# A convolution layer on one core: its first row transfers on another queue, the next chunk's loads ahead of them, and its accumulating stores issued later in the program

## The chip, the core and the metric

The kernel runs on one core of a Trainium2 chip. The metric is the time of one execution on the device in microseconds (us); smaller is better. The core has TensorE (PE in the profile, its weight loads PEld), VectorE (DVE), ScalarE (ACT), GpSimd (POOL) and SyncE (SP). SP, ACT and POOL can issue transfers (DMAs). In the profile "SPq" or "POOLq" is the queue of that engine, and "L1160" is line 1160 of the kernel.

## The reference

The input `x` holds 1024 pictures of 16 x 16 positions with 16 channels. Four layers of the form `x = x + layer(groupnorm(x))` follow one another: a tensor-train matrix product (layer 0), a small cellular automaton with a hidden layer of 128 (layer 1), a 3 x 3 convolution (layer 2), and a second automaton (layer 3). The change is in layer 2:

```python
def _L2_conv_ref(x, filters, bias):
    out = jax.lax.conv_general_dilated(x, filters, window_strides=(1, 1),
        padding='SAME', dimension_numbers=('NHWC', 'HWIO', 'NHWC'))
    return out + bias

x = x + _L2_conv_ref(_gn(x), L2_conv_filters, L2_conv_bias)
```

## The kernel before

**Chunks.** The batch is cut into two chunks of 512 pictures. Two large buffers in SBUF, `X0` and `X1` (128 partitions x 32 lines x 512 pictures), hold the normalized activations of a chunk. A layer runs on chunk 0 in `X0` and then on chunk 1 in `X1`. While one chunk is convolved, the other buffer is loaded with the input of the layer that comes next for it, and normalized in place. The residual stream lies in DRAM in the tensors `xf`.

**Layer 2 (`layer_conv`).** For chunk `n`, each of 16 rows `h` is computed in two halves `wh` of the row's width, as matmuls of 128 x 128 weights with up to three lines of `X` (`inner`, L1160). What crosses from one half to the other is added by `across` (L1169), whose operands are copied beforehand from `X` into small tiles `hx`. The function `halo(k)` (L1146) copies them for four rows: twelve rows of 16 partitions in six DMAs on SP's queue, and for `k = 0` also two small ones at L1156. `start()` issues `halo(0)`, and the rows 1, 5 and 9 issue the next ones. `finish(h)` (L1187) lets ACT add the bias while it moves each half of a row from PSUM to a tile `r` (L1191), of which there are six, and lets POOL issue a DMA at once that adds this tile to the residual stream in DRAM (L1192).

**Order of work.** Instructions are written in the program's order for each engine[...]. `run` (L1423) interleaves three lists: the 54 main steps of the convolution; the 16 loads of the other buffer (512 KB each), spread evenly until the share `by` of the main steps is done; and the steps of the normalization of that buffer, laid out between the shares `lo` and `hi` of the main steps, in proportion to their costs. What lies beyond the last main step is written at its end. So `by`, `lo` and `hi` only set the place of an instruction in the queues.

**The two runs of layer 2.** The first (L1536) convolves `X0` and loads and normalizes `X1` for the second; the loads come from the stream that layer 1 left, and the normalization is `norm_lines`: sums over all 16 pairs of lines (DVE L589, L592, L596), a matmul for the mean (L675), a copy of it by ACT (L636), 16 subtractions (DVE L621), squares (ACT L606) and their sum (DVE L592), a matmul for the variance (L679), a root (ACT L653) with a refinement on DVE (L659 to L663), and 16 multiplications (DVE L621). The second (L1538) convolves `X1` and loads and normalizes `X0` for layer 3 with `norm_cw`, which does the same in four quarters of eight lines each, interleaved: one mean (L704) and one variance (L708) for each quarter, then one root and, for each quarter, a matmul that spreads it (L720), a copy (L636) and four multiplications. These loads read what the first run's accumulating DMAs write, and each of them needs all 16 rows of its half. Before them `put(L3)` (L1455) loads the weights of layer 3.

**Transfers in flight.** [...]

Of the kernel before, what the change touches and what calls it, by code (L numbers as in the profile page):

```python
# [12 lines left out]
ALU = mybir.AluOpType  # L13
# [90 lines left out]
def conv_preact_kernel(ctx: ExitStack, tc: tile.TileContext, a: dict, out: bass.AP):  # L104
    nc = tc.nc
    V, A, G, T = nc.vector, nc.scalar, nc.gpsimd, nc.tensor
# [9 lines left out]
    xf = [  # L116
        [dram.tile([8, 4, P, NB], F32, tag=f"xf{l}_{n}", name=f"xf{l}_{n}") for n in range(NCH)]
        for l in range(5)
    ]
# [16 lines left out]
    def work(shape, tag, name, dt=F32):  # L136
        p, sizes = pool["sb"]
        return p.tile(shape, dt, tag=tag, name=name, bufs=sizes[tag])
# [5 lines left out]
    def psum(shape, name):  # L144
        return bank(shape, shared[0], name)
# [485 lines left out]
    def held(st, q=0):  # L631


        def copy():
            st["m", q] = work([P, NB], "s", "m")
            A.copy(st["m", q], st["p"])  # L636

        return (0, copy)
# [28 lines left out]
    def norm_lines(X, on_act=True):  # L667
        parts = [lambda l=l: X[:, l : l + 2] for l in range(0, NL, 2)]
        s1, steps = line_sum(parts, "s1", False)
        s2, more = line_sum(squares(X, 0, NL, on_act), "s2", True, not on_act)  # L670
        st = {}

        def mean():
            st["p"] = psum([P, NB], "pmean")
            T.matmul(st["p"], gm_wc, s1["s"], start=True, stop=True)  # L675

        def var():
            st["v"] = psum([P, NB], "pvar")
            T.matmul(st["v"], gm_wc, s2["s"], start=True, stop=True)  # L679

        def keep():
            st["ve"] = work([P, NB], "n", "ve")
            V.tensor_scalar(st["ve"], st["v"], GN_EPS, None, ALU.add)

        steps = steps + [5, mean, 2, held(st), 2] + each(X, 0, NL, lambda: st["m", 0], ALU.subtract)
        steps += more + [5, var, 2, keep] + rstd(st)
        return steps + by_rows(each(X, 0, NL, lambda: st["r"], ALU.mult))
# [49 lines left out]
    def norm_cw(X, on_act):  # L737


        st, N = parts_cw(X, on_act)  # L740
        sums, sq, hold = N["sums"], N["sq"], N["held"]
        mean, var, keep, spread = N["mean"], N["var"], N["keep"], N["spread"]
        steps = sums[0] + woven(sums[1], (2, mean[0]), (3, hold[0])) + [1] + sq[0]
        for q in (1, 2):
            steps += woven(
                sums[q + 1], (1, var[q - 1]), (3, keep[q - 1]), (3, mean[q]), (4, hold[q])
            ) + [2] + sq[q][:4]
            if q == 1:
                steps += sq[q][4:]
        steps += woven(sq[2][4:], (2, mean[3]), (3, hold[3]))  # L750
        steps += woven(sq[3], (2, var[2]), (4, keep[2])) + [5, var[3], 2, keep[3]]
        return steps + rstd(st) + [4] + scaled(N, range(4))
# [11 lines left out]
    def load_wc(X, src):  # L764
        return [
            lambda wh=wh, h=h: nc.sync.dma_start(X[:, 16 * wh + h : 16 * wh + h + 2], rows_wc(src, wh, h, 2))
            for wh in range(2)
            for h in range(0, S, 2)
        ]

    def load_cw(X, src):
        return [
            lambda q=q, w=w: nc.sync.dma_start(
                X[:, 8 * q + w : 8 * q + w + 2], src[w : w + 2, q].rearrange("w p b -> p w b")
            )
            for q in range(4)
            for w in range(0, 8, 2)
        ]
# [5 lines left out]
    def rows_wc(t, wh, h, n=1):  # L784

        t = t[4 * wh : 4 * wh + 4].rearrange("w q (c h) b -> (w q c) h b", h=S)
        return t[:, h : h + n]
# [349 lines left out]
    def layer_conv(X, n):  # L1137

        st = {}

        def start():
            halo(0)

        def halo(k):  # L1146
            t = st["h", k] = work([P, 4, NB], "hx", "hx")
            for wh in range(2):
                src = X[slice(97, 128, 2) if wh else slice(0, 32, 2), 16 * (1 - wh) : 16 * (1 - wh) + 16]
                for y in range(3):  # L1150
                    r0, h0 = 64 * wh + 16 * y, 4 * k + y - 1
                    lo, hi = max(h0, 0), min(h0 + 4, S)
                    nc.sync.dma_start(t[r0 : r0 + 16, lo - h0 : hi - h0], src[:, lo:hi])
                    if lo > h0:

                        nc.sync.dma_start(t[r0 : r0 + 16, 0:1], src[:, 0:1])  # L1156

        def inner(h, y):
            for wh in range(2):
                T.matmul(  # L1160
                    st["po", h][wh], conv["fw"][:, y], X[:, 16 * wh + h + y - 1],
                    start=y == max(0, 1 - h), stop=y == min(2, S - h),
                )

        def across(h):
            rows = 32 if h == S - 1 else 48
            for wh in range(2):
                cols = slice(0, 32) if wh else slice(96, 128)
                T.matmul(  # L1169
                    st["po", h][wh][cols], conv["hw"][64 * wh : 64 * wh + rows, h == 0],  # L1170
                    st["h", h // 4][64 * wh : 64 * wh + rows, h % 4], start=False, stop=False,
                )

        def first(h):
            if h % 2 == 0 and h > 0:
                finish(h - 1)
            if h % 4 == 1 and h + 4 < S:
                halo(h // 4 + 1)
            st["po", h] = [bank([P, NB], "o", "po2") for _ in range(2)]
            inner(h, max(0, 1 - h))  # L1180

        def last(h):
            inner(h, min(2, S - h))
            if h % 2 == 0 or h == S - 1:
                finish(h)

        def finish(h):  # L1187

            for wh in range(2):
                r = work([P, NB], "r", "conv")  # L1190
                A.activation(r, st["po", h][wh], AF.Identity, bias=b2)  # L1191
                G.dma_start(rows_wc(xf[2][n], wh, h), r.unsqueeze(1), accum_op=ALU.add)  # L1192

        steps = []
        for h in range(0, S, 2):
            for j in (h, h + 1):
                steps.append(lambda j=j: first(j))
                if 0 < j < S - 1:
                    steps.append(lambda j=j: inner(j, 1))
            steps += [  # L1200
                lambda h=h: (across(h), across(h + 1)), lambda h=h: last(h), lambda h=h: last(h + 1)
            ]
        return start, steps

    def layer_nca(X, n, l, L, xo=None):
# [217 lines left out]
    def run(layer, us, loads, *spans, by=0.0):  # L1423

        start, main = layer
        start()
        loads, done = list(loads), 0  # L1430
        todo = []
        for bg, lo, hi in spans:
            bg = [b if isinstance(b, tuple) else (1, b) if callable(b) else (b, None) for b in bg]
            idle = sum(b[0] for b in bg if b[1] is None) / (us * (hi - lo))
            less = min(1.0, 0.7 / idle) if idle else 1.0
            weight = sum(b[0] for b in bg if b[1] is not None)
            at = lo
            for cost, step in bg:
                if step is None:
                    at += cost * less / us  # L1440
                else:
                    todo.append((at, step))
                    at += (hi - lo) * (1 - idle * less) * cost / weight
        todo.sort(key=lambda x: x[0])
        for i, step in enumerate(main):
            step()
            part = (i + 1) / len(main)
            while done < len(loads) and done < len(loads) * part / (by or 1e-9):
                loads[done]()
                done += 1  # L1450
            while todo and (todo[0][0] < part or i == len(main) - 1):
                todo.pop(0)[1]()

    def put(L):
        return lambda: nc.sync.dma_start(pack, L["pack"])  # L1455

    X0, X1 = XN
    gn = dict(t4=3, s=3, n=2)
# [16 lines left out]
    L3, make3 = nca_weights("L3_conv_", X1[:, 16:32])  # L1475
# [42 lines left out]
    last = alone(N, 3) + rstd(nst, slice(96, 128)) + [3] + scaled(N, [3])  # L1518
    nca_sb = dict(t4=2, s=3, n=2, wq=5, mask=1, f=5, hid=8, u=2, r=4, nx=1)
    nca_ps = dict(h=6, o=2)  # L1520
    conv_sb, conv_ps = dict(gn, s=3, r=6, hx=3), dict(o=6, m=2)
    on_vector[0] = True
    with ExitStack() as es:
        shared[0] = "o"
# [8 lines left out]
    with ExitStack() as es:  # L1533
        shared[0] = "m"
        stage(es, conv_sb, conv_ps)
        run(layer_conv(X0, 0), 108, load_wc(X1, xf[2][1]), (norm_lines(X1), 0.09, 1.1), by=0.12)  # L1536
        run(
            layer_conv(X1, 1), 108, [put(L3)] + load_cw(X0, xf[3][0]), (norm_cw(X0, True), 0.09, 1.04), by=0.12  # L1538
        )
    with ExitStack() as es:  # L1540
        shared[0] = "o"
# [41 lines left out]
```

## Time and profile before

| what | value |
|---|---|
| time, median of three runs | 3199.06 us (3191.19, 3199.06, 3200.33) |
| the profiled execution | 3191.8 us |
| its span, first to last instruction | 3190.1 us |
| PE busy | 3058.5 us (96%) |
| DVE, ACT, POOL busy | 1785.6, 1018.3, 670.6 us |
| mean granted clock of PE | 0.98 |
| layer 2, first run (PE, 2339.7 to 2464.0 us) | 124.3 us, PE busy 105.1, DVE 78.9, ACT 37.4; DMA share 0.78 |
| layer 2, second run (PE, 2464.0 to 2591.5 us) | 127.5 us, PE busy 111.6, DVE 79.6, ACT 41.1; DMA share 0.72 |
| the 64 accumulating DMAs (L1192) | 256 KB each, 0.87 us of POOL each to issue, 6.1 us to landing (median) |

"DMA share" is the mean busy share of the core's 16 DMA engines. All times inside the execution count from the start of its span. The limits of the two runs are those of PE's own matmuls: from the first matmul of row 0 to the first matmul of what follows.

### The profile page before, as it was taken

How to read it: one execution, taken by the hardware profiler on the slowest of the kernel's cores; microseconds unless marked ns; L12 is line 12 of the kernel's file. 1: busy time of each engine (PE TensorE's matmuls, PEld its weight loads, DVE VectorE, ACT ScalarE, POOL GpSimd, SP SyncE). 2: the span in 40 equal slices, each digit the busy share in tenths (PEclk: the TensorE clock that was granted, in tenths of full speed). 3: DMA queues.
4: the chain of work that ended last, by engine and by line, in shares of the span. 5: the costliest groups of instructions: out<-in, count | busy, mean ns of one | idle time of the engine just before them, and what ended most of it. 6: DMA issues, size and time to landing. Idle time of an engine off the chain costs nothing.

```text
span 3190.1 us, 37179 instructions
## 1 busy us (share of the span) xinstructions
PE 3058.5 (96%) x13874; PEld 1260.3 (40%) x13874; DVE 1785.6 (56%) x2378; ACT 1018.3 (32%) x1690; POOL 670.6 (21%) x706
## 2 busy tenths in 40 slices
PE   7899899999999999999999999999979899999996
PEld 5444333444444444444444433333323233333332
DVE  5255345755554555544556678558757647754222
ACT  4331221100001000000111166666624356655553
POOL 1116532200000000000000034435432124432221
PEclk8999999999999999999999999999989999999998
DMA  7535545443333433322222254454476765433445
GB/s 283 201 142 97 121 101 160 133 144 104 104 109 132 146 116 104 104 98 96 90 95 90 76 168 133 129 167 154 139 192 110 185 139 173 136 92 115 128 137 186
DMA packets 243299, 424.77 MB, mean 133 GB/s; under 512 B 37844, under 2 KB 91952, under 8 KB 239408
## 3 DMA queue, kind: packets, MB, share of 16 engines
q1 hardware_dynamic: 217824, 368.63, 35.5%
q0 software_dynamic: 24480, 53.48, 8.3%
q8 instruction: 110, 1.80, 0.2%
q14 instruction: 69, 0.57, 0.1%
q10 hardware_dynamic: 816, 0.30, 0.0%
HBM read 238.78 MB, written 165.60 MB: 127 GB/s over the span
## 4 chain that ended last, share of the span: by engine, by line
issue 46%; PE 31%; POOL 8%; DMA 4%; DVE 2%; SPq 1%; ACT 1%; POOLq 0%; DVEq 0%; ACTq 0%
PE ph L1410 11%; PE po L1078 10%; PE po L1263 4%; POOL res L1313 4%; POOL u L1312 4%; PE po L1160 2%; DMA xn<-xf 1%; PE L_conv_pe L382 1%; SPq L941 1%; DVE xn L621 1%; DMA hx<-xn 1%; PE pw L1001 1%; PE ptout L948 1%; DVE sq L592 1%; POOL L_conv_wy L394 0%
## 5 line engine op out<-in xcount | busy, mean ns | idle before, releaser
L1078 PE MATMUL po<-xn,w 128*128 128x512 f32 x3584 | 1584.3, 598 | 4.6 <-DVE xn L892 4.6
L1078 PEld LDWEIGHTS po<-xn,w 128*128 128x128 f32 x3584 | 669.9, 190 | 852.6 <-issue 833.7
L1413 ACT ACTIVATE hid<-ph,pack 128x512 f32<-128x512 f32 x1024 | 653.9, 686 | 429.2 <-PE ph L1410 308.4
L1114 DVE TENSOR_TENSOR r<-r,po 128x512 f32<-128x512 f32 x576 | 377.8, 683 | 499.0 <-PE po L1078 476.3
L1312 POOL TENSOR_TENSOR u<-u,mask 128x512 f32<-128x512 f32 x128 | 202.5, 1582 | 1858.9 <-DMA nx<-xn 1241.7
L1410 PE MATMUL ph<-xn,wq 32*128 32x512 f32 x3664 | 573.1, 613 | 1.5 <-DMA wq<-L_conv_wy 1.5
L1006 ACT COPY w<-pw 128x512 f32<-128x512 f32 (+1 forms) x320 | 150.6, 558 | 1194.0 <-issue 970.4
L1410 PEld LDWEIGHTS ph<-xn,wq 32*128 32x128 f32 x3664 | 228.6, 184 | 263.3 <-issue 231.4
L1410 PE MATMUL ph<-xn,pack 32*128 32x512 f32 x1288 | 302.2, 631 | 4.5 <-ACT hid L1413 3.2
L1263 PE MATMUL po<-hid,pack 128*32 128x512 f32 x2048 | 283.0, 609 | 1.2 <-DVE u L1275 0.9
L1019 DVE TENSOR_TENSOR w<-w 128x512 f32<-128x512 f32 x320 | 211.2, 684 | 115.2 <-ACT w L1006 114.7
L621 DVE TENSOR_TENSOR xn<-xn,m 128x1024 f32<-128x1024 f32 x160 | 225.9, 1461 | 47.1 <-ACT m L636 47.1
L1313 POOL TENSOR_TENSOR res<-res,u 128x512 f32<-128x512 f32 x128 | 215.2, 1681 | 17.0 <-PE po L1263 2.7
L1275 DVE SCALAR_TENSOR_TENSOR u<-po,pack,xn 128x512 f32<-128x512 f32 x128 | 95.9, 749 | 157.6 <-PE po L1263 150.9
L1160 PE MATMUL po<-xn,convw 128*128 128x512 f32 x368 | 168.5, 609 | 0.0
L1410 PEld LDWEIGHTS ph<-xn,pack 32*128 32x128 f32 x1288 | 114.5, 187 | 100.7 <-issue 61.7
L1114 DVE TENSOR_TENSOR xn<-xn,po 128x512 f32<-128x512 f32 x96 | 64.3, 684 | 125.9 <-PE po L1078 125.8
L592 DVE TENSOR_TENSOR sq<-sq 128x1024 f32<-128x1024 f32 x78 | 110.6, 1418 | 15.2 <-ACT sq L606 12.0
L1263 PEld LDWEIGHTS po<-hid,pack 128*32 128x32 f32 x2048 | 42.9, 108 | 189.7 <-issue 137.4
L394 POOL DMA_DIRECT2D L_conv_wy<-xn x160 | 89.0, 563 | 99.0 <-ACT xn L152 90.7
L1160 PEld LDWEIGHTS po<-xn,convw 128*128 128x128 f32 x368 | 69.3, 193 | 99.3 <-issue 96.7
L592 DVE TENSOR_TENSOR s<-s,xn 128x1024 f32<-128x1024 f32 x60 | 86.4, 1441 | 29.1 <-DMA xn<-xf 27.9
(163 smaller groups left out, 1776.9 us busy)
## 6 DMA issues: line engine op xcount, KB each, us to landing
xf<-r SPq DMA_DIRECT2D x112, 512.0 KB, 3.8
xn<-xf SPq DMA_DIRECT2D x96, 512.0 KB, 5.1
r<-xf SPq DMA_DIRECT2D x80, 512.0 KB, 4.5
wq<-L_conv_wy SPq DMA_DIRECT2D x192, 192.0 KB, 2.8
res<-xf SPq DMA_DIRECT2D x128, 256.0 KB, 3.0
xf<-res SPq DMA_DIRECT2D x96, 256.0 KB, 2.0
res<-xr SPq DMA_DIRECT2D x256, 64.0 KB, 2.8
xf<-conv POOLq DMA_DIRECT2D x64, 256.0 KB, 6.1
```

Source lines behind the costliest of these rows:

```text
L592: return lambda: V.tensor_tensor(st["t"], st["t"], p(), ALU.add)
L621: V.tensor_tensor(part, part, m().unsqueeze(1).broadcast_to([P, 2, NB]), op)
L1006: A.copy(w[:, k0:4, :, 32 * r : 32 * r + 32].rearrange("p k t (v o) -> p v (k t) o", v=2), pw[r],)
L1019: V.tensor_tensor(w[:, k], w[:, x], w[:, y], ALU.add if sign > 0 else ALU.subtract)
L1078: T.matmul(po, st["w", u][:, matrix, t], x, start=t == 0, stop=t == 3)
L1114: V.tensor_tensor(r[at], r[at], po, ALU.add if sign > 0 else ALU.subtract)
L1160: T.matmul(st["po", h][wh], conv["fw"][:, y], X[:, 16 * wh + h + y - 1], start=y == max(0, 1 - h), stop=y == min(2, S - h),)
L1263: T.matmul(po[32 * j : 32 * j + 32], nca["w1"][:, v], hid[j], start=v == 0, stop=v == 1)
L1312: G.tensor_tensor(u, u, st["m"][:, w2], ALU.mult)
L1313: G.tensor_tensor(r, r, u, ALU.add)
L1410: T.matmul(ph, w, x, start=k == 0, stop=k == len(tiles) - 1)
L1413: A.activation(h, ph, AF.Relu, bias=nca["bt"][:, r : r + 1])
```

## The change

- `halo(0)` of each of the two runs is issued from ACT's queue and no longer from SP's. The later ones stay on SP.
- `finish(h)` no longer writes the accumulating DMAs behind the bias at once. It puts them into a list. Those of row 0 and 1 are written into POOL's queue when row 5 is finished, then four at each of the rows 5 to 9, and from row 10 on two at each row. There are twelve tiles `r` and not six.
- The loads are written within the first 7% of the main steps and not 12%.
- In the second run `put(L3)` stands behind the 16 loads and not ahead of them.
- The normalization of the first run is laid out up to 1.08 and not 1.10, that of the second up to 1.10 and not 1.04.

```diff
         def start():
-            halo(0)
+            halo(0, A)
-        def halo(k):
+        def halo(k, queue=nc.sync):
...
-                    nc.sync.dma_start(t[r0 : r0 + 16, lo - h0 : hi - h0], src[:, lo:hi])
+                    queue.dma_start(t[r0 : r0 + 16, lo - h0 : hi - h0], src[:, lo:hi])
                     if lo > h0:
-                        nc.sync.dma_start(t[r0 : r0 + 16, 0:1], src[:, 0:1])
+                        queue.dma_start(t[r0 : r0 + 16, 0:1], src[:, 0:1])
...
+        waiting = []
         def finish(h):
             for wh in range(2):
                 r = work([P, NB], "r", "conv")
                 A.activation(r, st["po", h][wh], AF.Identity, bias=b2)
-                G.dma_start(rows_wc(xf[2][n], wh, h), r.unsqueeze(1), accum_op=ALU.add)
+                waiting.append((rows_wc(xf[2][n], wh, h), r.unsqueeze(1)))
+            while waiting and 2 * h + 2 - len(waiting) < 4 * (h - 4):
+                G.dma_start(*waiting.pop(0), accum_op=ALU.add)
...
-    conv_sb, conv_ps = dict(gn, s=3, r=6, hx=3), dict(o=6, m=2)
+    conv_sb, conv_ps = dict(gn, s=3, r=12, hx=3), dict(o=6, m=2)
...
-        run(layer_conv(X0, 0), 108, load_wc(X1, xf[2][1]), (norm_lines(X1), 0.09, 1.1), by=0.12)
+        run(layer_conv(X0, 0), 108, load_wc(X1, xf[2][1]), (norm_lines(X1), 0.09, 1.08), by=0.07)
         run(
-            layer_conv(X1, 1), 108, [put(L3)] + load_cw(X0, xf[3][0]), (norm_cw(X0, True), 0.09, 1.04), by=0.12
+            layer_conv(X1, 1), 108, load_cw(X0, xf[3][0]) + [put(L3)], (norm_cw(X0, True), 0.09, 1.1), by=0.07
         )
```

## The prediction

> **What bounds the kernel now.** I read the page first: PE is busy 96% of the span, so what can be won is what PE waits. Then the waits of PE in the stretch of layer 2 (2330 to 2600 us):
>
> ```profile
> PE pmean L675 <- DVE s1s L596: 12.4, 1, 12.4
> PE pmean L704 <- DVE s1s L596: 11.0, 1, 11.0
> PE po L1169 <- DMA hx<-xn: 6.2, 2, 5.4
> PE pvar L708 <- DVE s2s L596: 4.9, 2, 2.6
> PE pvar L679 <- DVE s2s L596: 0.6, 1, 0.6
> ```
>
> 35 us in all: twice PE stands at the mean of the other chunk's normalization, because DVE has not summed all lines, and at the start it stands for the halo. Why is DVE late? Its timeline in the first run:
>
> ```profile
> 2364.43 2.50 DVE L592 TENSOR_TENSOR s<-s,xn 128x1024 f32<-128x1024 f32 x2 [5.88 <-DMA xn<-xf]
> 2368.18 1.22 DVE L592 TENSOR_TENSOR s<-s,xn 128x1024 f32<-128x1024 f32 x1 [1.25 <-DMA xn<-xf]
> ...
> 2391.78 1.22 DVE L592 TENSOR_TENSOR s<-s,xn 128x1024 f32<-128x1024 f32 x1 [1.43 <-DMA xn<-xf]
> ```
>
> It waits for loads. Eleven loads (6th to 16th) take 2391.8 - 2365.7 = 26.1 us, 2.37 each. The stretches of time say why (the last three columns are PE's granted clock, DMA share and GB/s):
>
> ```profile
> 2345.00:2350.00 5.00, 0.11 (x1) 0.00 (x0) 0.00 (x0) 0.00 (x0) 0.00 (x0) 1.00 0.79 180
> 2350.00:2355.00 5.00, 3.69 (x7) 0.69 (x8) 0.00 (x0) 0.00 (x0) 0.00 (x0) 0.52 0.93 249
> 2365.00:2370.00 5.00, 5.00 (x16) 1.85 (x16) 3.10 (x3) 0.00 (x0) 0.00 (x0) 1.00 1.08 308
> 2490.00:2495.00 5.00, 4.06 (x5) 1.85 (x6) 3.96 (x5) 0.58 (x1) 0.00 (x0) 0.50 1.04 387
> ```
>
> The DMA engines are full. Loads alone (last line) run at 387 GB/s, 1.35 us for 512 KB; the eight accumulating DMAs of rows 0 to 3 took 18.6% of the 16 engines over 61 us (queues in 2339 to 2400), 1.42 each; 11 x 1.35 + 8 x 1.42 = 26.2, the 26.1 seen. A halo is about 0.79 x 5 us = 4.0 of DMA time (first line, an upper estimate). Last, the queues that issue:
>
> ```profile
> 2343.17 1.27 POOL L1313 TENSOR_TENSOR res<-res,u 128x512 f32<-128x512 f32 x1
> 2359.87 0.95 POOL L1192 DMA_DIRECT2D xf<-conv  x1 [15.44 <-ACT conv L1191]
> 2361.58 2.61 POOL L1192 DMA_DIRECT2D xf<-conv  x3 [0.77 <-ACT conv L1191]
> 2373.02 3.50 POOL L1192 DMA_DIRECT2D xf<-conv  x4 [8.83 <-ACT conv L1191]
> ```
>
> Between layer 1's last multiply-add and layer 3, POOL has nothing but these DMAs, and each goes out about 0.3 us after the ACT instruction that fills its tile (the first ran 2358.87 to 2359.56).
>
> [...]
>
> **The change, part by part.**
>
> *Held rows.* The code only moves the 20 DMAs of rows 0 to 9 later in program order. POOL's queue holds nothing between them. Each waits for its own tile, not for row 5: that a wait is for the needed work alone, and not for all that is written earlier, is seen at the second run's first halo, written behind all 16 multiplications (L621): it went out at 2454.99, after the fourth, 13 us ahead of the last. So POOL should reach the DMA of row 0 as early as before, and issue it when its tile is filled: **no row is held**, 0 us. The 8 x 1.42 = 11.4 us of contention stay. Were rows held, they would go (first rival). Twelve tiles in place of six remove no wait: none of ACT's idle time was for a tile.
>
> *First halo by ACT, first run.* SP stood behind the last stores (L1315) until 2344.78. ACT is free at 2338.7, but the tile `hx` is the first one of its pool and takes the place of layer 1's first, the mask, last read by POOL until 2343.1. So the eight issues start at 2343.2, between bounds of 2338.7 and 2344.9: 1.7 earlier. Issues took 0.57 each on SP (2344.87 to 2349.82 for eight less the last); ACT's 16 of the start of the kernel took 0.32 to 0.56. I take 0.6 with waits. The last lands some 1 us earlier at best, since loads now run beside it; PE's 6.2 us shrink by 0 to 1.7. That is worth nothing yet, for PE stands later at the mean.
>
> *Loads first.* Loads may start as the halo DMAs before them land (eight in flight), from 2345.8 and not 2349.86, five of them ahead of `halo(1)` instead of three. DMA engines fill 1.3 us sooner (0.79 and 0.93 become 1 in two stretches) and the halo begins 1.7 sooner: total work is the same, so the last load lands 3 us earlier, at 2388.5, and PE's mean comes at 2390.6 instead of 2393.9: **-3.3 us**. PE stood there from 2381.4 before, now from 2380.7 or so: 10 us of wait stay.
>
> *1.08 in the first run.* Laying the steps out by their costs, the variance (0.768 before, 0.754 now, of 54 steps) stands one step earlier, ahead of `first(12)` (4 passes of 0.44 us). PE waits for DVE's sum there (0.57 before), so the step it had done before the wait comes after it: **+1.8**. DVE's chain sum, subtract, square is continuous and moves by -3.3. Run 1 ends at T = 2464.0 - 3.3 + 1.8 = 2462.5.
>
> *First halo by ACT, second run.* SP issued it from 2454.99 on, as soon as DVE had multiplied the rows, 14 us before PE needed it (2469.28). ACT comes to it only behind the bias of row 15, 1.0 us after T (2463.43 to 2464.98 before). Behind it on ACT is nothing until `finish(0)`. Eight issues take 4.9 us; the DMAs share the engines with the last four accumulations (5.7 us): together about 9.7 us, so they land near T + 10.5, while PE needs them at T + 5.3: a **new wait of about 5 us**, with a half-clock start that I put at 0 to 2.5 us.
>
> *Loads of the second run.* They wait for the last accumulations (2470.5 before, T + 6.5). The halo delays these by 1 to 4 us, `put(L3)`, moved behind, gives about 1 back; I take T + 7.8 = 2470.3, as before. Four loads of the first quarter now go together: 2.3 + 4 x 1.35 + 1, then 2.3 us of DVE: first sum at 2481 (before 2490.9). PE reaches the mean at T + 5.3 + 5 + 1.8 + 8.8 + 1 = 2484.4: **the 11.0 us go**. What is late next: the second quarter. DVE subtracts only after its sum, and loads 5 to 8, `halo(1)` and the accumulations of rows 0 and 1 are the same work as before: 8 x 1.35 + 4.0 + 5.7 = 20.5 us, with 2.3 to the first landing and 2.3 of DVE, so this ends near 2495.4 against 2496.2. Squares then save 2.7 (before, ACT stood behind row 2's bias until 2499.69): variance at 2505.2 against 2507.9. PE arrives at 2498: **a new wait of 7 us**. The gain of the mean is handed on to the variance.
>
> *1.10 in the second run.* The first two variances stand one step later (0.278 against 0.264), so PE has one step more behind it: -1.8. From the first variance to the second DVE, ACT and PE alternate: 16.9 us, as before (17.05), plus 2.5 if PE restarts at half clock. I take it: second variance at 2524.6 (before 2524.9). The rest, 66.5 us before, is 64.8: PE ends at 2589.4 (before 2591.5). The spreads move three steps later (0.829 to 0.875), so the third quarter's multiplications start only after the last row's bias; layer 3's first matmuls need the first of them some 1.3 us after PE's end: +1.
>
> **Sum:** -2.1 + 1 = about -1; with no half-clock restart -3.5. I take -2: 3191.8 - 2 = 3190 for an execution like the profiled one, whose span is 1.7 us less. The median lies 7.3 above it, and the three runs stand at two levels, so the same -2 gives 3197 there; I write 3195. A measurement of this kernel can tell about 0.3%, 9.6 us.
>
> **The rivals.**
> - *Rows are held after all* (POOL meets a wait that I don't see). For: it is what the edit is meant to do. Against: POOL's empty queue. Then loads run alone: run 1's mean at 2380.7, -13; the second quarter's sum 5.7 plus about 4 sooner: in all -20, 3172 to 3179. Chance 0.10.
> - *Slower.* The halo of the second run goes ahead of the last accumulations in full, 4 us, so all loads and DVE's chain come 4 us later, and run 1 gains nothing while its +1.8 stays, and +1.3 at layer 3: +7, with a cold start +9.6; 3199 to 3207. It decides from accumulations that land later than T + 10. For: both lists of DMAs are issued in the same 4 us. [...] Chance 0.20.
> - *Lighter DMA.* The halo is an upper estimate; if it costs 2.5 us and PE stays warm, -8, 3184 to 3191. Chance 0.10.
> - My forecast, -6 to +3: 0.60.
>
> Faster by over 0.3%: 0.10 and 0.04 of the third; slower: 0.12 of the second and the forecast's edge; the rest, 0.74, within. The range 3182 to 3206 leaves out held rows and the ends of the others.
>
> **What would show it.** Right: POOL's first L1192 near 2359 and not after row 5; the mean of run 1 at 2390; the halo wait in run 2 at 5 us, L704 no longer waiting, L708 waiting 7. Wrong: POOL's first L1192 after 2385 with loads at 1.35 us each.

## The result, and the profile after

The changed kernel takes 3199.35 us in the median of four runs (3198.74 to 3201.45), the kernel before beside it 3198.85 in four: the ratio is 1.0008, with an interval of 0.999 to 1.0025. This measurement cannot tell it from no change. I had said 3195, and had given 0.74 to a change of less than 0.3%. The total is as forecast; the way there is not.

PE's waits in layer 2 of the changed kernel (2330 to 2610 us; line, what it waited for, us in total, times, longest):

```profile
PE po L1169 <- DMA hx<-xn: 31.7, 4, 13.9
PE pvar L708 <- DVE s2s L596: 3.2, 2, 2.2
PE pvar L679 <- DVE s2s L596: 2.2, 1, 2.2
PE ph L1414 <- DVE xn L621: 1.1, 1, 1.1
```

The 23.4 us of waits at the two means (L675, L704) are gone. But `across` (L1169) now waits 31.7 us for its halo, and had waited 6.2. The sum of all waits is 38.2 us against 35.1. PE's timeline has the four waits, and behind them the means that no longer wait:

```profile
2360.23 1.91 PE L1169 MATMUL po<-hx,convw 48*32 48x512 f32 x2 [13.86 <-DMA hx<-xn]
...
2365.26 3.59 PE L1169 MATMUL po<-hx,convw 48*32 48x512 f32 x6 [3.11 <-DMA hx<-xn]
...
2393.07 1.02 PE L675 MATMUL pmean<-s1s,gm_wc 128*128 128x512 f32 x2
...
2473.94 1.50 PE L1169 MATMUL po<-hx,convw 48*32 48x512 f32 x2 [4.13 <-DMA hx<-xn]
...
2486.05 3.59 PE L1169 MATMUL po<-hx,convw 48*32 48x512 f32 x6 [10.62 <-DMA hx<-xn]
...
2500.85 1.02 PE L704 MATMUL pmean<-s1s,gm_cw 128*128 128x512 f32 x2
```

The halo waits are 17.0 us in the first run and 14.75 in the second. I had forecast 4.5 to 6.2 and 5. ACT's queue in the first run (start, length):

```profile
2344.39 0.60 ACTq L1153 DMA_DIRECT2D hx<-xn  x1
2345.02 0.59 ACTq L1156 DMA_DIRECT2D hx<-xn  x1
2345.66 7.83 ACTq L1153 DMA_DIRECT2D hx<-xn  x3
2353.52 0.60 ACTq L1156 DMA_DIRECT2D hx<-xn  x1
2354.16 4.73 ACTq L1153 DMA_DIRECT2D hx<-xn  x2
```

ACT starts when I said, but eight issues of 0.6 us take until 2358.9: within the group of three (its third to fifth) it stands some 6 us, in the last pair (its seventh and eighth) 3.5. Meanwhile SP has issued five loads in 2.6 us, from 2346.13 on. And POOL, whose queue was to hold the rows, issues the first of them:

```profile
2371.93 0.95 POOL L1196 DMA_DIRECT2D xf<-conv  x1 [26.23 <-ACT conv L1193]
```

ACT's first bias ended at 2371.62; POOL issued 0.31 us later. No row is held.

### The profile page after: what moved, and what is told of

It reads as the page before. It is cut to its first block, busy times and chain, and to the rows that moved or that the text cites. A ratio compares the mean times of both kernels' runs of the same rounds, so it can differ in the third digit from the quotient of the medians.

```text
span 3197.5 us, 37179 instructions
## 1 busy us (share of the span) xinstructions
PE 3063.8 (96%) x13874; PEld 1261.1 (39%) x13874; DVE 1785.4 (56%) x2378; ACT 1018.0 (32%) x1690; POOL 669.7 (21%) x706
## 4 chain that ended last, share of the span: by engine, by line
issue 49%; PE 30%; POOL 9%; DMA 3%; SPq 1%; DVE 1%; ACT 0%; POOLq 0%; DVEq 0%; ACTq 0%
PE ph L1414 11%; PE po L1078 9%; PE po L1267 4%; POOL u L1316 3%; POOL res L1317 3%; PE po L1160 2%; PE L_conv_pe L382 1%; DMA L_conv_wy<-xn 1%; POOL xf L1196 1%; SPq L941 1%; PE ptout L948 1%; PE po L1169 1%; PE pw L1001 1%; POOL L_conv_wy L394 0%; PE ptx L1326 0%
## 5 line engine op out<-in xcount | busy, mean ns | idle before, releaser
L1414 PE MATMUL ph<-xn,wq 32*128 32x512 f32 x3664 | 574.4, 614 | 1.4 <-DMA wq<-L_conv_wy 1.4
L1414 PEld LDWEIGHTS ph<-xn,wq 32*128 32x128 f32 x3664 | 228.7, 184 | 263.0 <-issue 232.0
L1414 PE MATMUL ph<-xn,pack 32*128 32x512 f32 x1288 | 304.4, 633 | 5.8 <-ACT hid L1417 3.6
L1414 PEld LDWEIGHTS ph<-xn,pack 32*128 32x128 f32 x1288 | 114.9, 187 | 102.2 <-issue 62.5
L592 DVE TENSOR_TENSOR sq<-sq 128x1024 f32<-128x1024 f32 x78 | 110.7, 1419 | 16.4 <-ACT sq L606 13.1
L592 DVE TENSOR_TENSOR s<-s,xn 128x1024 f32<-128x1024 f32 x60 | 86.6, 1443 | 21.5 <-DMA xn<-xf 20.1
```

The costliest lines, as they stand in the source:

```text
L592: return lambda: V.tensor_tensor(st["t"], st["t"], p(), ALU.add)
L1414: T.matmul(ph, w, x, start=k == 0, stop=k == len(tiles) - 1)
```

## The experiments

Twelve kernels, each against the kernel before. A profiled execution's whole time is a poor witness here: row 0 of layer 2 began anywhere from 2334.3 to 2345.5 us, though none of the edits touches the layers ahead of it. So the table has, beside the ratio of times, the length of layer 2 from its first `inner` to its last, and PE's waits in it (what layer 3 waits at its start, up to 1.1 us, is not counted). The same kernel, profiled twice (e4, e8), differed there by 3.3 us, so a smaller difference of two rows says nothing. The waits are in us; "halo" is L1169, "means" L675 and L704, "variances" L679 and L708.

| kernel | ratio of times, interval | layer 2 | halo | means | variances | sum |
|---|---|---|---|---|---|---|
| before | 1 | 251.8 | 6.2 | 23.4 | 5.5 | 35.1 |
| changed | 1.0008 [0.999, 1.0025] | 254.6 | 31.7 | 0 | 5.4 | 37.1 |
| e1, halo on SP | 0.9989 [0.9982, 0.9997] | 250.3 | 6.2 | 16.0 | 11.2 | 33.4 |
| e2, before + halo on ACT | 0.9991 [0.9985, 0.9998] | 252.0 | 27.6 | 0 | 5.4 | 33.0 |
| e3, rows held | 1.0003 [0.9996, 1.0011] | 254.9 | 30.6 | 0 | 6.2 | 36.8 |
| e4, rows held, halo on SP | 0.9938 [0.9916, 0.996] | 233.7 | 6.1 | 1.7 | 12.3 | 20.1 |
| e5, halo on POOL | 0.9999 [0.9989, 1.001] | 254.2 | 21.4 | 3.9 | 5.2 | 30.5 |
| e6, before + rows held | 0.9928 [0.9912, 0.9945] | 235.2 | 6.2 | 7.0 | 7.4 | 20.6 |
| e7, e4 + nine loads ahead | 0.9908 [0.9893, 0.9922] | 226.0 | 6.2 | 1.7 | 7.4 | 15.3 |
| e8, e4 again | 0.9939 [0.9923, 0.9955] | 237.0 | 6.2 | 2.9 | 13.4 | 22.5 |
| e9, five loads on POOL | 0.9998 [0.9989, 1.0006] | 251.1 | 28.8 | 0 | 5.4 | 34.2 |
| e10, before + loads first | 1.0001 [0.9991, 1.001] | 252.4 | 6.2 | 13.5 | 16.4 | 36.1 |
| e11, e6 + loads first | 0.9936 [0.9916, 0.9956] | 236.2 | 6.2 | 1.9 | 14.5 | 22.6 |
| e12, e9 + second halo on POOL | 1.0113 [1.0096, 1.013] | 292.0 | 68.9 | 0 | 5.4 | 74.3 |

My theory after the result: the halo DMAs on ACT's queue stand until DMAs of SP's queue, loads above all, have landed, because both take the same eight semaphores in turn; and what the means win, the halo loses. In the changed kernel's trace the 1852 DMAs that SP and ACT issue in the whole execution carry eight semaphores, numbered 100 to 107, and POOL's 388 carry eight others, 111 to 118. Of SP's and ACT's, 1844 follow another on their semaphore, and each of these was issued after that one had landed. In the kernel before it is the same, and there the numbers come in turn at 1848 of 1851 steps. The rival: the loads ahead fill the DMA engines, whatever queue the halo is on.

### e1 and e2: the two halves of the change

e1, the changed kernel with one edit:

```diff
-            halo(0, A)
+            halo(0)
```

> The changed kernel with one part undone: the first halo is issued by SP again. Theory (the first halo on ACT's queue is what takes back the gain, because each of its DMAs shares a semaphore in turn with a 512 KB load on SP and so waits for it): PE's wait for halos falls from 31.7 us to about 6 in the first run and 0 in the second; some 10 us of wait at the first run's mean come back, the second run's mean costs 0 to 2, its first variance 7 to 10; in all 3 to 6 us faster than the changed kernel. Rival (the order of loads and the new layout of the normalization eat the gain): halo wait falls all the same, but the time stays within 2 us of the changed kernel.

e2, the kernel before with one edit:

```diff
-            halo(0)
+            halo(0, A)
```

> The kernel before with one part alone: the first halo is issued by ACT; loads, layout and accumulating DMAs as before. Theory (semaphores shared in turn with loads): PE waits 15 us or more for halos in each run although fewer loads stand ahead, and the time is 3 to 10 us longer than before. Rival (only the five loads ahead delay it, by taking the DMA engines): the halo waits are 6 to 9 us in the first run and 5 in the second as predicted, and the time is within 2 us of before.

e1 came out 0.2% under the changed kernel, as expected, though the two intervals overlap. e2 did not do what was expected: its halo waits nearly as long as forecast (13.4 and 14.3 us, where 15 or more was expected and the rival had 6 to 9 and 5), yet the kernel is as short as e1. The waits of the means, 23.4 us, have gone. While PE stands at the halo, DVE's loads go on, and the rows and their accumulations start later; so the sums are ready when PE gets to the mean. A wait of the halo doesn't add to a wait of the mean, it takes its place. Each half alone gains 0.1% in the median time, both together nothing; in the profiles, layer 2 of e1 and e2 is within the 3.3 us of before.

### e3, e4 and e8: rows really held

One column of a row's tile is read by POOL before it issues, so that its queue stands until that row's bias (45.02 us in e4's timeline below, with the four DMAs of the list behind it):

```diff
+            if 5 <= h < 10:
+                G.tensor_copy(seen, r[:, 0:1])
             while waiting and 2 * h + 2 - len(waiting) < 4 * (h - 4):
                 G.dma_start(*waiting.pop(0), accum_op=ALU.add)
```

e3 is the changed kernel with this; e4 has `halo(0)` on SP besides; e8 is e4 once more.

> The changed kernel, in which GpSimd now copies one column of the tile of row 5 (then 6 to 9) before it issues the DMAs that the list frees at that row, so that rows are truly held. Theory (no row is held in the changed kernel, and in it loads no longer bound PE, the halo does): the first accumulating DMA goes out after row 5, the loads run at 1.35 us each, yet PE still waits some 30 us for halos: 0 to 5 us faster. Rival (contention of the accumulations is what counts): 12 us or more faster.

> The same true holding, and the first halo on SP again. Theory: both causes are gone; PE waits about 6 us for the first run's halo and none in the second, none to 3 at the means, up to 8 at the variances: 12 to 22 us faster than before. Rival (the load stretch is bound by something else than the accumulations, and the gain of holding was never there): 3 to 6 us faster, as with the halo on SP alone.

> The kernel with held rows and the halo on SP a second time, beside the kernel with nine loads ahead on the same chip, since those two are to be compared to some 2 us. Expected as in its first run: 0.992 to 0.996 of the kernel before; if the gain of 20 us was the chip's and not the kernel's, 0.998 or more.

POOL's timeline in e4:

```profile
2389.81 1.13 POOL L1197 COPY seen<-conv 128x1 f32<-128x1 f32 x1 [45.02 <-ACT conv L1194]
2390.89 3.58 POOL L1199 DMA_DIRECT2D xf<-conv  x4
```

Now the first accumulation goes out 50.8 us after row 0's start at 2340.06 (31.0 in the changed kernel), when DVE's sum over the loads has ended. The four longest of PE's waits in e4:

```profile
PE pvar L709 <- DVE s2s L597: 8.8, 2, 6.5
PE po L1170 <- DMA hx<-xn: 6.1, 2, 5.4
PE pvar L680 <- DVE s2s L597: 3.5, 1, 3.5
PE pmean L705 <- DVE s1s L597: 1.2, 1, 1.2
```

The kernel of e4 and e8 is 0.6% faster than before, both times, and 18.1 and 14.8 us shorter in layer 2. e3 holds the rows as well, and gains nothing: there PE waits 30.6 us for a halo on ACT, not for loads, and a lighter load of the engines at the mean is worth nothing.

### e5, e9 and e12: semaphores or bandwidth?

e5 takes ACT's queue and its semaphores out of it; POOL's DMAs have the eight others (111 to 118 in the changed kernel):

```diff
-            halo(0, A)
+            halo(0, G)
```

> The changed kernel with the first halo issued by POOL's queue in place of ACT's; everything else as in the changed kernel. [...] Theory (the halo is late because its DMAs on ACT's queue wait, in the shared row of eight semaphores, until loads of SP's queue have landed): PE's wait for the halo falls from 17.0 us in the first run to 7 to 9, and from 14.75 in the second to about 8; the waits of PE's means come back in part. Rival (it is late because five loads of 512 KB lie ahead of it on the same engines, whatever queue issues it): it stays at 13 us or more in the first run and 12 or more in the second. The time: 3190 to 3199 in either case, since the waits of layer 2 have so far only changed places (33 to 38 us in all).

The first run fell between the two bands, the second near the first theory's. PE in e5:

```profile
2360.91 1.88 PE L1169 MATMUL po<-hx,convw 48*32 48x512 f32 x2 [10.04 <-DMA hx<-xn]
...
2364.92 3.59 PE L1169 MATMUL po<-hx,convw 48*32 48x512 f32 x6 [2.13 <-DMA hx<-xn]
...
2483.92 1.88 PE L1169 MATMUL po<-hx,convw 48*32 48x512 f32 x2 [5.21 <-DMA hx<-xn]
...
2489.83 3.59 PE L1169 MATMUL po<-hx,convw 48*32 48x512 f32 x6 [4.03 <-DMA hx<-xn]
```

The waits are 12.2 and 9.2 us. POOL had issued all eight DMAs of the first run by 2354.0, and PE could go on at 2360.9: the five loads were in flight beside them. So 12.2 - 6.2 = 6.0 us of the first run's 17.0 stay without ACT's queue, and 4.8 go with it. I put the 6.0 down to the shared engines; that POOL's way of issuing adds nothing to them is not shown. In the first run POOL starts 1.2 us later after row 0 than ACT did, so the part of the semaphores may be larger by that much. In the second run the difference is 14.75 - 9.2 = 5.5 us, and too small as a measure: there POOL's sixth, seventh and eighth DMA of the halo waited 1.1, 0.8 and 1.0 us for accumulations of its own queue to land (`<-DMA xf<-conv`).

In e9 the halo stays on ACT and the first five loads go to POOL:

```diff
-            lambda wh=wh, h=h: nc.sync.dma_start(
+            lambda wh=wh, h=h: (G if 8 * wh + h // 2 < ahead else nc.sync).dma_start(
...
-        run(layer_conv(X0, 0), 108, load_wc(X1, xf[2][1]), ...
+        run(layer_conv(X0, 0), 108, load_wc(X1, xf[2][1], 5), ...
```

and the same in the second run.

> The changed kernel with the first five loads of each run, those that stand ahead of the second halo, issued by POOL's queue in place of SP's; the halo stays on ACT's. Now no semaphore of the shared eight lies between a halo DMA and a load ahead of it, and the bytes that share the DMA engines are the same. Theory A (the halo DMAs on ACT wait for these loads to land, and that is most of the delay): PE's wait for the halo falls to 9 us or less in each run. Theory B (as the kernel with the halo on POOL hints: the five loads and the halo share the engines and end together, whichever queue issues them): it stays at 10 us or more in each, and only some 5 us of the 17.0 and 14.75 are the semaphores'. The time in either case 3190 to 3200, for what the halo gives back the means take.

The second run did as theory A says: 4.39 + 2.35 = 6.7 us, 8 less than in the changed kernel; but there POOL issued its loads only from 2475.89 on, when ACT's eight DMAs were nearly all out (the last pair from 2474.79), so that engines were shared less as well. The first went the other way, to 22.1: ACT's sixth DMA stood 8 us. The first DMA of the second halo, on SP, was issued at 2344.95 and landed 9.9 us later; ACT's sixth left at 2354.88. I read it as the same semaphore, given to the one on SP first. e12 moves that halo to POOL, too:

```diff
         def halo(k, queue=nc.sync):
+            queue = G if k == 1 else queue
```

> As the kernel with the first five loads on POOL's queue, and the second halo on POOL's queue too: in that kernel the sixth of the halo DMAs on ACT waited 8 us, since the semaphore that it shares with the first DMA of the second halo on SP had been dealt to that one first. Now nothing on SP stands before a halo DMA of ACT in the row of semaphores, except stores that have landed. The bytes are the same. Theory A (the order of the shared semaphores is most of the delay): ACT issues its eight DMAs without a gap of more than 2 us, and PE's wait for the halo is 9 us or less in each run (6 without loads beside it). Theory B (shared engines are most of it): ACT has no gap, yet the wait is 12 us or more in the first run. Between 9 and 12 both count, and the gap's share of the 17.0 us is what is missing. The time stays at 3190 to 3200.

ACT's queue in e12, first run:

```profile
2343.30 0.60 ACTq L1154 DMA_DIRECT2D hx<-xn  x1
2343.94 0.59 ACTq L1157 DMA_DIRECT2D hx<-xn  x1
2344.57 11.02 ACTq L1154 DMA_DIRECT2D hx<-xn  x3
2355.64 0.61 ACTq L1157 DMA_DIRECT2D hx<-xn  x1
2371.26 3.26 ACTq L1154 DMA_DIRECT2D hx<-xn  x2
```

and SP's:

```profile
2345.06 21.76 SPq L766 DMA_DIRECT2D xn<-xf  x11
```

I was wrong about what would stand on SP: with its queue free, the other eleven loads go out from 2345.06 on, and I read the times as semaphores dealt to them between those of ACT's DMAs. The sixth of these loads was issued at 2351.86 and landed 19.4 us later, at 2371.3; ACT's seventh DMA left at 2371.26, over 15 us after its sixth. PE waits 34.7 and 34.2 us, and the kernel is 1.1% slower. So the clean split of the 17 us, which e12 was for, it doesn't give; that a load on SP's queue stops ACT's queue it shows best of all. How the two share in the first run rests on e5 alone.

### e6, e10, e11 and e7: what each part is worth alone

e6 is the kernel before with rows really held (list, twelve tiles, the copy of e3) and nothing else.

> The kernel before with one thing added: the accumulating DMAs of rows 0 to 9 are really held in POOL's queue until row 5 (POOL copies one column of the tile of each of the rows 5 to 9 before it issues), with twelve tiles. The halo on SP ahead of the loads, the loads until 12%, the weights of layer 3 ahead of the loads, 1.10 and 1.04 are as before. Theory (most of what the kernel with held rows and SP's halo won is the contention of eight accumulations with the loads in each run): 12 to 18 us shorter than before, PE's waits for the means gone but for 3 us. Rival (the layout of the steps and the earlier loads carry half of it): 5 to 10 us shorter, with a wait for a mean of 5 us or more left in the second run.

e10 is the kernel before with the loads' order alone, the spans as before:

```diff
-(norm_lines(X1), 0.09, 1.1), by=0.12)
+(norm_lines(X1), 0.09, 1.1), by=0.07)
...
-[put(L3)] + load_cw(X0, xf[3][0]), (norm_cw(X0, True), 0.09, 1.04), by=0.12
+load_cw(X0, xf[3][0]) + [put(L3)], (norm_cw(X0, True), 0.09, 1.04), by=0.07
```

> The kernel before with the loads' order alone: loads within 7% of the main steps and the weights of layer 3 behind them; the halo on SP, no row held, and the spans 1.10 and 1.04 as before. If the spans 1.08 and 1.10 cost what I said (1.8 us for the first, a win of 1.8 and a loss of 1 for the second), this runs 1 us shorter than the kernel with these spans too, 0.998 to 0.999 of before, and PE's wait for the variance of the first run is 0.6 us again in place of 2.2. If the spans do nothing, the wait is 2 us or more here as well.

e11 is e6 with that order.

> The kernel with rows really held and nothing else, with the loads' order added: loads within 7% and the weights of layer 3 behind them; the spans 1.10 and 1.04 as before. If the earlier loads are worth something once the contention is gone, PE's wait of 6.4 us for the mean of the second run falls below 2 and the time is 3 to 5 us under that of the kernel that only holds rows (0.991 to 0.992 of before). If the waits only change places again, the variances of the second run take these 6 us and the time is 0.993 to 0.994.

e6 alone has the whole gain of e4: 0.72% or 21.7 us, more than expected, though in layer 2 it is 16.6 us, between those of e8 and e4; and 7.0 us of waits for the means stay. In its first run the mean came 2376.70 - 2334.29 = 42.4 us after row 0; before, 2393.86 - 2339.70 = 54.2. The loads' order alone moves waits, as PE's waits of e10 show:

```profile
PE pvar L708 <- DVE s2s L596: 15.9, 2, 13.2
PE pmean L675 <- DVE s1s L596: 12.4, 1, 12.4
PE po L1169 <- DMA hx<-xn: 6.2, 2, 5.4
PE pmean L704 <- DVE s1s L596: 1.1, 1, 1.1
PE pvar L679 <- DVE s2s L596: 0.5, 1, 0.5
```

Mean and variance of the second run cost 11.0 + 4.9 = 15.9 before and 1.1 + 15.9 = 17.0 here. The same with held rows: 6.4 + 4.9 in e6, 1.4 + 11.9 in e11, and the time is that of the expectation's second branch, no gain. As to the spans: with 1.10, L679 waits 0.5 us (e10), with 1.08, 2.2 (e1): that cost is real where no row is held (with held rows and 1.10 the same wait is 2.5 us in e6 and 3.3 in e7). But e10 did not come out 1 us shorter than e1, nor at 0.998 to 0.999 of before: its layer 2 is 2.1 us longer than that of e1, less than two profiles of one kernel differ by, so what the two spans do together stays open.

e7 asks where e4's last long wait comes from, the second quarter's loads behind the second halo:

```diff
-(norm_lines(X1), 0.09, 1.08), by=0.07)
+(norm_lines(X1), 0.09, 1.1), by=0.07)
...
-(norm_cw(X0, True), 0.09, 1.1), by=0.07
+(norm_cw(X0, True), 0.09, 1.07), by=0.035
```

> The kernel with held rows and the halo on SP, with three numbers changed: the loads of the second run within 3.5% of the main steps (so nine in place of five stand ahead of the second halo), its normalization laid out up to 1.07 and not 1.10, that of the first run up to 1.10 and not 1.08. Theory (what PE still waits for the first variance of the second run, 6.5 us, is the second quarter's loads standing behind the second halo; what it waits for the variance of the first run, 3.5 us, is the earlier place of that step): the two waits fall to about 1 and 2 us, the one at layer 3's start goes; 8 us shorter than the kernel with held rows and SP's halo. Rival (these waits move on to the next quarter or to the second halo, as the waits of layer 2 have done so far): within 2 us of it.

On the same chip e7 took 3167.24 us and e8 3176.9: 9.7 less, with 8 expected. The longest wait for a variance of the second run fell from 7.0 (e8) to 2.8; L680 hardly moved, so its 3.3 us are not the 1.08. Three numbers were changed at once, and which of them carries the gain no run tells apart. e7 is the fastest kernel here, 0.9908 of before.

## Why the prediction held in its total and failed in three steps

- **Held rows: right.** "POOL's first L1192 near 2359 and not after row 5": 2371.93, 0.31 us behind its bias, and late only because PE was. e6 shows what the edit would have been worth.
- **The first rival, -20 if rows are held: right in size.** e4 is the changed kernel but for the copies and the queue of the halo: -18.1 us in layer 2 (-14.8 in e8). The 11.4 us of contention that I had summed match the 54.2 - 42.4 = 11.8 us by which the mean of the first run came earlier in e6. What I didn't see is that the rival needs the halo back on SP (e3).
- **First halo by ACT, first run: this step failed.** I had its start at 2343.2; with row 0 1.26 us later, 2344.46, and 2344.39 it was. (SP's issues before followed one another every 0.62 us, not 0.57; I took 0.6, so nothing hangs on it.) But "PE's 6.2 us shrink by 0 to 1.7" became 17.0. I had counted on eight DMAs of SP and ACT in flight, used it for the loads ("as the halo DMAs before them land"), and took it that the halo's DMAs come first in the row because they are first in the program. They were dealt between DMAs of SP: in the trace ACT's fourth has the semaphore of the second load (100), its fifth that of the third (102), and its eighth that of the first DMA of the second halo (107). The times agree: these three landed at 2351.6, 2352.9 and 2358.3, and ACT's three left at 2351.74, 2352.97 and 2358.38. A smaller part is a mis-sized term: I put the halo at 4.0 us of the full engines, "an upper estimate". Its packets took 5.2 us of the 16 engines here (17.3% of 2340 to 2370), beside loads; in e4, where it goes ahead of them, 3.4 (a DMA share of 0.67 from 2345 to 2350). The stretches of time of the changed kernel in which almost only the two halos pass (last three columns as before: PE's clock, DMA share, GB/s):

```profile
2356.00:2358.00 2.00, 0.00 (x0) 0.00 (x0) 0.46 (x1) 0.00 (x0) 0.00 (x0) 0.50 1.04 138
2358.00:2360.00 2.00, 0.00 (x0) 0.00 (x0) 0.76 (x1) 0.00 (x0) 0.00 (x0) 0.50 1.11 153
2360.00:2362.00 2.00, 1.77 (x2) 0.18 (x2) 0.00 (x0) 0.00 (x0) 0.00 (x0) 0.50 1.21 148
```

  The engines are full at 146 GB/s (the mean of the three), where loads run at 387. At that rate a halo of 0.79 MB costs 5.4 us.
- **Loads first, -3.3 us: this step failed, too.** DVE's sum of the first run, in the changed kernel and before:

```profile
2388.06 0.69 DVE L596 TENSOR_TENSOR s1s<-s 128x512 f32<-128x512 f32 x1
...
2393.11 0.69 DVE L596 TENSOR_TENSOR s1s<-s 128x512 f32<-128x512 f32 x1
```

  It ended 2388.75 - 2340.96 = 47.8 us after row 0, and 2393.80 - 2339.70 = 54.1 before: 6.3 earlier, about double of what I had summed. But the loads' order did not do it. PE's mean before, and in e1, which has the order without the halo on ACT:

```profile
2393.86 2.08 PE L675 MATMUL pmean<-s1s,gm_wc 128*128 128x512 f32 x2 [12.41 <-DVE s1s L596]
...
2395.46 2.08 PE L675 MATMUL pmean<-s1s,gm_wc 128*128 128x512 f32 x2 [12.42 <-DVE s1s L596]
```

  That is 54.2 us after row 0 before and 54.1 in e1 (row 0 at 2341.34); 54.3 in e10. In e2, which has the halo on ACT and the old order, the sum ended 45.7 us after row 0. So the gain comes with the halo on ACT: SP is free for the loads 5 us earlier, and PE's late rows issue their accumulations later; which of the two counts for more is not shown. "10 us of wait stay" at the mean failed for the same reason: PE came later than the sum. The first run in all took 123.5 us (124.3 before): -0.8, where I had summed -1.5.
- **1.08, +1.8: right.** L679 waits 2.2 instead of 0.6.
- **First halo by ACT, second run: the third step that failed; the halo wait is 14.75, not "about 5".** ACT came to it where I said, right behind T (2464.5), but its third, fourth and fifth issues lasted 10.4 us. Its fifth has the semaphore of the first load (102), which itself had to wait for the accumulations: issued at 2471.97, it landed at 2476.0, and ACT's fifth left at 2475.99. That wait is what "together about 9.7 us, so they land near T + 10.5" leaves out; the halo's size was not the error here, for its packets took 3.3 us of the engines (13.8% of 2464 to 2488). How the engines divide themselves between two queues was my estimate in that figure, and no run here tests it: ACT's last four DMAs were issued only from 2475.99 on. The half-clock start, an estimate of mine too (0 to 2.5 us), did come: PE's granted clock was 0.50 from 2475 to 2490.
- **L704's 11.0 us go, "the gain of the mean is handed on to the variance": right as a mechanism.** e10 shows it pure. In the changed kernel the halo, earlier in the line, took it instead, and L708 waits 3.2 and not 7.
- **1.10 and layer 3, +1: right,** 1.1 us at L1414.

The total was right because two misses cancel. That they cancel is not luck alone: all kernels that neither hold rows nor put SP's queue ahead of ACT's as e12 does have 30.5 to 37.1 us of waits in layer 2, whatever queue and order they use. My reading is that the DMA engines have the same work to pass in the same stretch, and PE waits for it at one place or another. It is argued, not shown, and it is not the whole: e3 has less work in the stretch and still waits 36.8 us, for its halo on ACT. How closely they cancelled here was luck: the steps had foreseen neither. The second rival, in which the halo goes ahead of the last accumulations and all loads come 4 us later, didn't come about: the loads of the second run began 7.5 us after T (2471.97), where I had 7.8. The 2.8 us by which layer 2 is longer are less than two profiles of one kernel differ by.

## What to carry to other kernels

Where several waits of the bound engine hang on one full resource, sum them: here the edits that only reordered the transfers moved the wait from one consumer to the next (30.5 to 37.1 us in all, e12 aside), until work was taken out of the stretch (eight accumulations, by a queue that must really stand). After that a new order was worth something, too: e7 is 9.7 us faster than e8. A list in the program didn't delay a queue that was empty (POOL issued 0.31 us behind the bias, and in e4, with something to wait for, 50.8 us after row 0); give it something to wait for. And before a DMA goes to a "free" queue, look at which semaphores it shares and what is dealt ahead of it: here a small transfer on one queue stood behind large ones of another (ACT's fourth left at 2351.74, when the second load of 512 KB on SP had landed at 2351.6).

## What the runs showed of the hardware that I had not expected

- Transfers of 16 partitions within SBUF can fill the DMA engines at 128 to 153 GB/s (2360 to 2365 us in e4 and the lines above), 33 to 40% of what loads of 128 partitions move at the same share (387 in the lines of before). But the first halo of e4 moved 157 GB/s at a share of 0.67 (2345 to 2350), so it cost less per byte. Of its packets 301 of 333 are under 8 KB, from 2360 to 2365 108 of 172; whether that is the reason no run tests.
- An idle stretch of PE of about 2 us was followed by its half clock in one kernel and not in another. After the wait of 2.21 us at L679 the changed kernel's next 16 passes took 8.73 us with a clock of 0.50 from 2441 to 2443; in e9, after 2.22 us at the same place, 7.03. In e5, after 2.00 us, the 16 took 8.09, slow as well; in e7, after 3.32 us, 12 passes took 5.31. In the kernel before, PE stood 5.39 us for the first halo, and its clock was 0.52 from 2350 to 2355 and 0.50 from 2355 to 2360. What decides between the outcomes no run here tests.
